# A transformer block with conditioned norms: the order of loads, modulation and first products in the first stage

## The chip, the cores and the metric

The kernel runs on one core of a Trainium2 chip. A core has TensorE (PE in the profile, with its weight loads as PEld), VectorE (DVE), ScalarE (ACT), GpSimd (POOL) and SyncE (SP), which here only issues transfers. Each engine takes its instructions in a fixed order that is set when the kernel is compiled; semaphores hold an instruction until what it needs is there. The metric is device time in microseconds, the median of several runs.

## What is computed

One transformer block on x of shape (2, 2048, 512) in float32, with 16 heads of 32 and a hidden width of 2048. A condition of 512 numbers per batch row makes six vectors (two shifts, two scales, two gates) that modulate both norms and gate both branches.

```python
mod = jax.nn.silu(condition) @ Wada + bada
sh_a, sc_a, gt_a, sh_m, sc_m, gt_m = jnp.split(mod, 6, axis=1)
xm = _layernorm(x, g1, be1) * (1.0 + sc_a[:, None, :]) + sh_a[:, None, :]
x = x + gt_a[:, None, :] * _attention(xm, Wqkv, Wproj, bproj)     # causal, 16 heads
xm = _layernorm(x, g2, be2) * (1.0 + sc_m[:, None, :]) + sh_m[:, None, :]
h = jax.nn.gelu(xm @ W1 + b1, approximate=False)
x = x + gt_m[:, None, :] * (h @ W2 + b2)
```

## The kernel before

The kernel goes through batch row 0 (queries, keys and values, then attention), batch row 1 the same way with row 0's projection among it, and then the feed-forward part for all tokens. The change is in the first stage, the queries, keys and values of row 0, nearly all of it in the work ahead of the first product.

**Groups and products.** Tokens come in groups `g` of 512 (`MT`), four 128-token tiles (`MTT`) each. The features of queries and keys come in four blocks `f` of 128. A product of tokens with weights is split in two halves each way and made with seven quarter products instead of eight; their names are A11, A12, A21 (also S4), A22, S1, S2, S3. The seven need sums of weight blocks (`weight_sum`, on POOL, L944) and sums of token halves (`token_sum`, on DVE, L997). The first unit, group 0 and f = 0, is made plainly instead, by `plain`: two sums of four N = 512 matmuls, one for queries and one for keys, so that it needs no sums (`ps_qk` in the profile). `Qkv.run` then goes through the units; after each step it calls `tick`, which prepares the next group (its token tiles' loads, stats, scaling, transposes) at set steps, and `also`, which a caller gives it.

**From tokens to xmT.** `load_x` (L919) loads a group's four token tiles on SP's queue. `stats` (L218, L221, on DVE) makes mean and variance of a tile; after the last of a group, `inv_std` makes a square root on ACT (L224) and, on DVE, its reciprocal (L225) and the shift (L226). `scaled` (L964, on ACT) normalises each tile in place. `norm` gives two tiles, half a group, to `transposed`, which transposes them on TensorE (L214, `ps_xt`) and returns `modulate`: it applies scale `a1` and shift `c1` while it writes `xmT`, even chunks on DVE (L269) and odd ones on ACT (L274).

**The modulation.** Seven small transfers on ACT's queue (L1373) bring the condition, the norms' gains and the biases as rows of one tile, `rows`; one transpose makes columns of it (`ps_c`, copied to `cols`, L1402). ACT makes Silu of the condition's columns (`sc`, L1455). `load_wada` brings two of the six slices of Wada as eight transfers on SP's queue (L1391) and their bias on POOL's. `modulation` multiplies (`ps_mod`, PE), adds the bias (`mr`, L1425, DVE) and turns the rows into columns (`ps_modt`, PE; `mod`, L1434, DVE); `scale_shift` makes `a1` and `c1` of them (L1443, L1448).

**The order.** The program is written as a sequence, and a planner orders each engine's instructions by its own costs, save those that are wrapped in `act(...)`, `mm(...)` or `transpose(...)`, which stay in the order of the program among themselves. Transfers of one queue start in their order; SP's first entries are x (four), Wada (eight), Wqkv for queries and keys (four of 512 KB, L926), Wqkv for values (four, L936).

ACT holds one table of functions at a time: changing between Sqrt and Silu is an `ACT_TABLE_LOAD`. Before, Sqrt is loaded at L136 by a dummy, Silu at L1455, and Sqrt again at L224 for group 1.

Of the kernel before, what the change touches and what calls it, by code (L numbers as in the profile page):

```python
# [17 lines left out]
P = 128  # L18
# [9 lines left out]
def dit_block_kernel(  # L28
# [107 lines left out]
    nc.scalar.activation(first, eps, AF.Sqrt)  # L136
# [99 lines left out]
    def transposed(pool_, psum, xts, n0, mv, rstd, a, c, b, dst, xns=None, share=False):  # L236
# [28 lines left out]
        def modulate(chunks=range(C)):  # L265
            for k in chunks:
                src = banks[k // per][:, k % per, :]
                if k % 2 == 0 and (share or not by_act):
                    nc.vector.tensor_scalar(  # L269
                        dst[:, k, :], src,  # L270
                        a[:, k, b : b + 1], c[:, k, b : b + 1], ALU.mult, ALU.add,
                    )
                else:
                    nc.scalar.activation(  # L274
                        dst[:, k, :], src, AF.Identity,
                        bias=c[:, k, b : b + 1], scale=a[:, k, b : b + 1],
                    )

# [619 lines left out]
    class Qkv:  # L898
# [6 lines left out]
        def __init__(self, row, qp, psum):  # L905
            self.row, self.qp, self.psum = row, qp, psum
            self.xts, self.xmT, self.loads = {}, {}, []
            self.done = set()
            self.w = qp.tile([P, 7, HK, D], F32, tag="wqk", name="wqk")
            self.t = {  # L910
                n: qp.tile([P, HK, HALF_T], F32, tag=f"t{n}", name=f"t{n}")
                for n in (S1, S2, A22)
            }

        def load_x(self, g):
            xts = []
            for t in range(MTT):
                xt = self.qp.tile([P, D], F32, tag="x", name="x", bufs=4)
                nc.sync.dma_start(xt, x_rows(self.row.b * NT + g * MTT + t))  # L919
                xts.append(xt)  # L920
            self.xts[g] = xts
# [68 lines left out]
        def token_sum(self, g, n):  # L990
# [6 lines left out]
            nc.vector.tensor_tensor(o[n], x, y, ALU.subtract)  # L997
# [88 lines left out]
        def plain(self, g, f, hp):  # L1086


            xmT, steps = self.xmT[g], []
            for which in range(2):  # L1090
                box = []
                for k in range(C):
                    def run(which=which, k=k, box=box):
                        if k == 0:
                            box.append(self.psum.tile([P, MT], F32, tag="mm", name="ps_qk"))
                        n = BASE[2 * which + k // HK][0]
                        mm(
                            box[0], self.w[:, n, k % HK, f * P : (f + 1) * P], xmT[:, k, :],
                            start=k == 0, stop=k == C - 1,
                        )  # L1100
                        if k < C - 1:
                            return
                        hi, lo = self.hi_tile(hp), self.lo_tile(hp)
                        scale = HD**-0.5 if which == 0 else 1.0
                        nc.scalar.activation(hi, box[0], AF.Copy, scale=scale)
                        nc.vector.scalar_tensor_tensor(
                            lo, box[0], scale, hi.bitcast(F32), ALU.mult, ALU.subtract
                        )
                        self.stored(g, f, which, (hi, lo))
                    steps.append(run)  # L1110
# [27 lines left out]
        def run(self, hp, also, early=()):  # L1138
# [3 lines left out]
            for g in range(NG):  # L1142
                at = [0]

                def tick():
# [214 lines left out]
    with pool("wada") as wp, pool("qkv0") as qp, pool("hl0") as hp, pool(  # L1360
        "ps_qkv0", bufs=6, space=PSUM
    ) as ps_mm:
        rows = wp.tile([n_rows, P], F32, tag="rows", name="rows")
        for r, n, src in (
# [8 lines left out]
            nc.scalar.dma_start(rows[r : r + n, :], src)  # L1373
# [76 lines left out]
        for t in range(MTT):  # L1450
# [23 lines left out]
        def also(g, n):  # L1474

            if (g, n) == (0, 7):
# [850 lines left out]
```

## Time and profile before

| | |
|---|---|
| median of 3 runs | 2256.44 us (2254.54 to 2258.32) |
| profiled execution | 2256.73 us |
| its span | 2255.0 us |
| TensorE busy | 2211.3 us (98%) |
| VectorE / ScalarE / GpSimd busy | 1535.7 / 1004.6 / 1297.9 us |
| idle of TensorE until its first product of tokens | see the rows from 0 to 18.12 us in the prediction |

A row of the timeline gives the start in us from the span's start, the length in us, the engine (SPq, ACTq: the queue on which a transfer is issued), the line, the operation, what it writes and reads, and how many instructions are merged; in brackets stands the engine's idle time before and what ended it. A row of the windows gives a stretch, its length, the busy time of PE, PEld, DVE, ACT and POOL with their instructions, the clock granted to TensorE as a share of full, the mean busy share of the DMA engines and the GB/s they moved. A float32 matmul stands as two records.

### The profile page before, as it was taken

The numbers are of one execution on the slowest core, as the hardware profiler recorded it, in microseconds if no ns is written. First come the engines' busy times: TensorE is split into PE (matmuls) and PEld (weight loads), VectorE is DVE, ScalarE is ACT, GpSimd is POOL, SyncE is SP. The second block draws the span as 40 slices with busy tenths as digits, with TensorE's granted clock in tenths as the row PEclk, the third lists the DMA queues.
The fourth block names the chain that finished last, engine by engine and source line by source line (L and its number), as shares of the span: only waits on it lengthen the run. The fifth ranks groups of instructions, "written<-read, shape, count | busy, mean of one in ns | idle before, by whom it ended". The sixth has DMA issues, their size and how long they took to land.

```text
span 2255.0 us, 33464 instructions
## 1 busy us (share of the span) xinstructions
PE 2211.3 (98%) x12057; PEld 1432.2 (64%) x12057; DVE 1535.7 (68%) x3309; ACT 1004.6 (45%) x2012; POOL 1297.9 (58%) x807
## 2 busy tenths in 40 slices
PE   7999999999999999999999999999999999999998
PEld 6777555555543587855555555345787787688687
DVE  4668766777757666777577767663685586576576
ACT  4434555555564244365656555614322422332410
POOL 4253998998983695199989898444205204304210
PEclk9999999999999999999999999999999999999999
DMA  8877143231324799542324113363353354353433
GB/s 281 251 259 193 43 93 75 62 85 48 106 97 135 252 308 313 142 92 62 85 67 104 44 48 131 109 231 129 109 175 133 123 184 145 108 187 126 158 125 110
DMA packets 160510, 311.57 MB, mean 138 GB/s; under 512 B 16544, under 2 KB 48844, under 8 KB 158552
## 3 DMA queue, kind: packets, MB, share of 16 engines
q1 hardware_dynamic: 155488, 285.53, 41.8%
q0 software_dynamic: 4480, 23.36, 2.7%
q8 instruction: 95, 1.56, 0.3%
q14 instruction: 71, 0.58, 0.1%
q10 hardware_dynamic: 376, 0.55, 0.1%
HBM read 229.95 MB, written 87.29 MB: 141 GB/s over the span
## 4 chain that ended last, share of the span: by engine, by line
PE 89%; DVE 4%; DMA 2%; POOL 2%; ACT 1%; issue 1%; SPq 0%; DVEq 0%; ACTq 0%; POOLq 0%
PE ps_a L206 27%; PE st L206 18%; PE ps_b L206 12%; PE o L206 10%; PE s L206 9%; PE ps_c L206 4%; PE ps_o L206 4%; PE sm L206 3%; DVE junk L498 1%; POOL ee L695 1%; PE ps_xt L214 1%; DMA x<-in_x_dram 1%; ACT e L670 1%; DVE mx L504 1%; PE ps_o L214 1%
## 5 line engine op out<-in xcount | busy, mean ns | idle before, releaser
L670 ACT ACTIVATE e<-st 128x512 f32<-128x512 f32 (+1 forms) x1152 | 575.0, 579 | 362.4 <-PE st L206 321.3
L504 DVE TENSOR_REDUCE mx<-s 128x1 f32<-128x512 f32 x576 | 381.9, 686 | 199.0 <-PE s L206 197.9
L695 POOL TENSOR_TENSOR ee<-ee,e 128x2048 f32<-128x2048 f32 x106 | 485.8, 4583 | 10.3 <-ACT e L670 4.3
L206 PE MATMUL st<-qst,kst 128*128 128x512 f32 (+3 forms) x1280 | 408.7, 386 | 0.0
L206 PE MATMUL s<-kst,qst 128*128 128x512 f32 (+3 forms) x1046 | 382.2, 396 | 8.0 <-DVE mx L498 2.7
L206 PE MATMUL ps_a<-sum,w 128*128 128x256 f32 (+1 forms) x1088 | 328.8, 431 | 0.1
L206 PE MATMUL o<-e,vv 128*32 128x512 f32 (+3 forms) x2560 | 293.2, 537 | 0.3 <-POOL e L682 0.3
L206 PEld LDWEIGHTS st<-qst,kst 128*128 128x128 f32 x1280 | 228.5, 188 | 97.3 <-issue 65.7
L498 DVE CUSTOM_DVE_ANT_0 junk<-s,causal 128x128 bf16<-128x128 f32 (+3 forms) x470 | 220.7, 470 | 61.0 <-PE s L206 46.8
L1795 POOL TENSOR_TENSOR sum<-w 128x256 f32<-128x256 f32 x30 | 21.8, 727 | 397.1 <-DMA w<-w1d 203.1
L206 PEld LDWEIGHTS s<-kst,qst 128*128 128x128 f32 x1046 | 195.4, 189 | 72.4 <-DVE mx L504 15.4
L206 PEld LDWEIGHTS ps_a<-sum,w 128*128 128x128 f32 x1088 | 204.5, 190 | 40.1 <-issue 11.4
L695 POOL TENSOR_TENSOR ee<-e 128x2048 f32<-128x2048 f32 x42 | 192.5, 4583 | 43.5 <-ACT e L670 42.5
L206 PEld LDWEIGHTS <-sel 32*128 32x128 bf16 x1152 | 29.5, 91 | 197.0 <-issue 196.1
L2014 ACT ACTIVATE h<-h,cols 128x512 f32<-128x512 f32 x120 | 76.8, 710 | 136.3 <-DVE h L1716 136.3
L504 DVE TENSOR_REDUCE mx<-st 128x1 f32<-128x512 f32 x192 | 131.0, 682 | 0.5
L682 POOL TENSOR_SCALAR_AFFINE_SELECT e<-e 128x512 f32<-128x512 f32 x128 | 83.3, 669 | 67.2 <-ACT e L670 67.2
L206 PE MATMUL st<-fold,sel 32*128 32x512 bf16 (+1 forms) x1152 | 117.3, 372 | 1.2
L206 PEld LDWEIGHTS o<-e,vv 128*32 128x32 f32 x2560 | 59.1, 108 | 92.3 <-issue 72.8
L1716 DVE TENSOR_TENSOR h<-c,ps_b 128x256 f32<-128x256 f32 x90 | 37.9, 421 | 103.5 <-PE ps_b L206 103.0
L1066 POOL TENSOR_TENSOR lo<-lo,hi 128x512 fp32r<-128x512 f32 x32 | 40.7, 1274 | 114.2 <-ACT hi L1064 109.8
L206 PE MATMUL ps_b<-sum,w 128*128 128x256 f32 (+1 forms) x384 | 95.0, 383 | 0.0
(237 smaller groups left out, 3590.7 us busy)
## 6 DMA issues: line engine op xcount, KB each, us to landing
qst<-q SPq DMA_DIRECT2D x128, 256.0 KB
kst<-k SPq DMA_DIRECT2D x128, 256.0 KB
w<-w1d SPq DMA_DIRECT2D x32, 896.0 KB
w<-w2d SPq DMA_DIRECT2D x28, 1024.0 KB
w<-w2d SPq DMA_DIRECT2D x28, 768.0 KB
q<-hi SPq DMA_DIRECT2D x32, 256.0 KB
q<-lo SPq DMA_DIRECT2D x32, 256.0 KB
k<-hi SPq DMA_DIRECT2D x32, 256.0 KB
```

The lines of the kernel that those rows point to most:

```text
L206: return tc.keep_in_program_order(nc.tensor.matmul(*args, **kw))
L214: return tc.keep_in_program_order(nc.tensor.transpose(dst, src, ident[:n, :n]))
L498: nc.vector.tensor_tensor_reduce(junk[:, :w], x, causal[:, QB - w :], 1.0, MASKED, ALU.add, ALU.max, m,)
L504: self.vector(nc.vector.tensor_reduce(m, x, axis=AX.X, op=ALU.max))
L670: act(nc.scalar.activation(e4[:, h, :w], sts[h][:, :w], AF.Exp))
L682: nc.gpsimd.affine_select(d, d, pattern=[[0, HC], [1, P]], compare_op=ALU.is_ge, fill=0.0, base=0, channel_multiplier=-1,)
L695: act(nc.gpsimd.tensor_tensor(dst, x, y, ALU.add))
L1066: engine.tensor_tensor(lo, d, hi.bitcast(F32), ALU.subtract)
L1716: act(nc.vector.tensor_tensor(dst, x, y, ALU.add))
L1795: act(engine.tensor_tensor(dst, u, v, op))
L2014: nc.scalar.activation(d[j], d[j], AF.Gelu, bias=col(r_b1 + half * HF + fs[j], 1))
```

## The change

1. SP's queue: the first two token tiles, then Wada, then the other two token tiles, then the weights of queries and keys by halves of the columns (f = 0, 1, then f = 2, 3), eight transfers of 256 KB, then those of values.
2. The condition has a transfer and a tile of its own (`rows_c`), ahead of the other small ones, and a transpose of its own (`ps_1`). Silu is loaded first, by a dummy behind the small transfers, and Sqrt behind Silu's use.
3. TensorE makes 6 dummy transposes ahead of `ps_1` and 32 behind it, ahead of the modulation.
4. Group 0's statistics are closed after two tiles each (`at_once`). The first half is normalised, transposed and modulated ahead of the first products; the second half's transposes and xmT, and the token sums, come after the products of the first half.
5. `plain` goes over token halves: four N = 256 matmuls for queries and four for keys with the first half of the tokens, then the same with the second.
6. The order is held (`act`) for xmT's writers, the token sums of group 0 and the stats of group 1.

```diff
-    nc.scalar.activation(first, eps, AF.Sqrt)
...
         def modulate(chunks=range(C)):
...
+                if share:
+                    act(ins)
...
-        def load_x(self, g):
+        def load_x(self, g, lo=0, hi=MTT):
...
-        def load_w(self, queue):
+        def load_w(self, queue, f=slice(0, D)):
             for n, i, k in BASE:
                 act(
                     queue.dma_start(
-                        self.w[:, n], w_v[:, k * HK : (k + 1) * HK, i * D : (i + 1) * D]
+                        self.w[:, n, :, f],
+                        w_v[:, k * HK : (k + 1) * HK, i * D + f.start : i * D + f.stop],
                     )
                 )
...
-            if t == MTT - 1:
-                inv_std(mv1, rstd1, shift1, n0, n0 + MTT)
+            if t % self.at_once == self.at_once - 1:
+                inv_std(mv1, rstd1, shift1, n0 + t + 1 - self.at_once, n0 + t + 1)
...
-            xmT, steps = self.xmT[g], []
...
+            xmT, steps, box = self.xmT[g], [], {}
+
+            def run(j, which, i):
+                tok = slice(j * HALF_T, (j + 1) * HALF_T)
+                if (j, i) == (0, 0):
+                    box[which] = self.psum.tile([P, MT], F32, tag="mm", name="ps_qk")
+                for k in range(i * HK, (i + 1) * HK):
+                    n = BASE[2 * which + i][0]
+                    mm(
+                        box[which][:, tok],
+                        self.w[:, n, k % HK, f * P : (f + 1) * P], xmT[:, k, tok],
+                        start=k == 0, stop=k == C - 1,
+                    )
+                if (j, i) != (1, 1):
+                    return
...
+            for j in range(2):
+                for which in range(2):
+                    for i in range(2):
+                        steps.append(lambda j=j, which=which, i=i: run(j, which, i))
...
-                            self.stats(g + 1, n - 10)
+                            self.stats(g + 1, n - 10, g == 0)
...
-            nc.scalar.dma_start(rows[r : r + n, :], src)
+            if not r:
+                act(nc.scalar.dma_start(rows_c, src))
+            act(nc.scalar.dma_start(rows[r : r + n, :], src))
+        act(nc.scalar.activation(first, eps, AF.Silu))
...
-        qkv.load_x(0)
+        qkv.load_x(0, 0, HK)
         load_wada(0, 1)
-        qkv.load_w(nc.sync)
+        qkv.load_x(0, HK, MTT)
+        for f0 in (0, 2):
+            qkv.load_w(nc.sync, slice(f0 * P, (f0 + 2) * P))
...
-        ps_c = ps_mm.tile([P, n_rows], F32, tag="mm", name="ps_c")
-        transpose(ps_c, rows)
-        nc.vector.tensor_copy(cols[:, :n_rows], ps_c)
+        ps_w = ps_sp.tile([P, P], F32, tag="s", name="ps_w")
+
+        def busy(n):
+            for _ in range(n):
+                transpose(ps_w, ident)
+
+        busy(6)
+        ps_1 = ps_sp.tile([P, n_cond], F32, tag="s", name="ps_1")
+        transpose(ps_1, rows_c)
...
-        for t in range(MTT):
-            qkv.stats(0, t)
-        halves = [qkv.norm(0, 0, True)]
-
         act(
             nc.scalar.activation(
-                sc[:, :, :B], col(0, n_cond).rearrange("p (b c) -> p c b", c=C), AF.Silu
+                sc[:, :, :B], ps_1.rearrange("p (b c) -> p c b", c=C), AF.Silu
             )
         )
+        act(nc.scalar.activation(first, eps, AF.Sqrt))
+        busy(32)
+        qkv.at_once = 2
+        for t in range(2):
+            qkv.stats(0, t)
+        qkv.scaled(0, 0)
         picks()
         columns = modulation(0)
-        halves.append(qkv.norm(0, 1, True))
+        ps_c = ps_mm.tile([P, n_rows], F32, tag="mm", name="ps_c")
+        transpose(ps_c, rows)
+        nc.vector.tensor_copy(cols[:, :n_rows], ps_c)
         columns()
+        modulate = qkv.norm(0, 0, True)
         scale_shift(a1, c1, r_g1, r_be1, 0, 1)
-        for k in range(0, C, 2):
-            for modulate in halves:
-                modulate((k, k + 1))
-        for n in (S1, S2, A22):
-            qkv.token_sum(0, n)
+        modulate()
+        for t in range(2, MTT):
+            qkv.stats(0, t)
+        qkv.scaled(0, 1)
+        qkv.at_once = MTT
...
         def also(g, n):
 
+            if (g, n) == (0, 2):
+                qkv.norm(0, 1, True)()
+                for s in (S1, S2, A22):
+                    qkv.token_sum(0, s, True)
```

More of the change, by code (lines that the diff above doesn't have):

```diff
@@ L268, in modulate @@
                 if k % 2 == 0 and (share or not by_act):
-                    nc.vector.tensor_scalar(
+                    ins = nc.vector.tensor_scalar(
                         dst[:, k, :], src,
@@ L273, in modulate @@
                 else:
-                    nc.scalar.activation(
+                    ins = nc.scalar.activation(
                         dst[:, k, :], src, AF.Identity,
@@ L908, in __init__ @@
             self.done = set()
+            self.at_once = MTT
             self.w = qp.tile([P, 7, HK, D], F32, tag="wqk", name="wqk")
@@ L913, in __init__ @@
             }
-        def load_x(self, g):
-            xts = []
-            for t in range(MTT):
+        def load_x(self, g, lo=0, hi=MTT):
+            xts = self.xts.setdefault(g, [])
+            for t in range(lo, hi):
                 xt = self.qp.tile([P, D], F32, tag="x", name="x", bufs=4)
@@ L920, in load_x @@
                 xts.append(xt)
-            self.xts[g] = xts
-        def load_w(self, queue):
+        def load_w(self, queue, f=slice(0, D)):
             for n, i, k in BASE:
@@ L988, in operands, with token_sum @@
             }
-        def token_sum(self, g, n):
+        def token_sum(self, g, n, keep=False):
             o = self.operands(g)
@@ L996, in token_sum @@
             }[n]
-            nc.vector.tensor_tensor(o[n], x, y, ALU.subtract)
+            ins = nc.vector.tensor_tensor(o[n], x, y, ALU.subtract)
+            if keep:
+                act(ins)
         def bank(self, name):
@@ L1086, in plain @@
         def plain(self, g, f, hp):
-            xmT, steps = self.xmT[g], []
[L1090 to L1110, printed above, removed]
+            xmT, steps, box = self.xmT[g], [], {}
@@ new lines, in run @@
+            def run(j, which, i):
[11 more added lines that the diff above has]
+                    return
+                hi, lo = self.hi_tile(hp), self.lo_tile(hp)
+                scale = HD**-0.5 if which == 0 else 1.0
+                nc.scalar.activation(hi, box[which], AF.Copy, scale=scale)
+                nc.vector.scalar_tensor_tensor(
+                    lo, box[which], scale, hi.bitcast(F32), ALU.mult, ALU.subtract
+                )
+                self.stored(g, f, which, (hi, lo))
@@ L1363, in dit_block_kernel @@
         rows = wp.tile([n_rows, P], F32, tag="rows", name="rows")
+        rows_c = wp.tile([n_cond, P], F32, tag="rowsc", name="rowsc")
         for r, n, src in (
```

1 line of the change is left out of this document (removed).

## The prediction

> **What bounds the kernel now.** I read the page first, then the instructions in order of time up to 50 us, then windows of the clock and of the DMA engines.
>
> ```profile
> span 2255.0 us, 33464 instructions
> PE 2211.3 (98%) x12057; PEld 1432.2 (64%) x12057; DVE 1535.7 (68%) x3309; ACT 1004.6 (45%) x2012; POOL 1297.9 (58%) x807
> PE 89%; DVE 4%; DMA 2%; POOL 2%; ACT 1%; issue 1%; SPq 0%; DVEq 0%; ACTq 0%; POOLq 0%
> ```
>
> TensorE (PE) carries 89% of the chain, so a late start of its steady work moves the end by as much. The change touches only the stretch before that. Its rows, all engines:
>
> ```profile
> 0.81 2.38 SPq L919 DMA_DIRECT2D x<-in_x_dram  x4
> 1.41 0.29 POOL masks.py:199 TENSOR_SCALAR_AFFINE_SELECT ident<-ident 128x128 f32<-128x128 f32 x1
> ...
> 4.22 3.79 SPq L1391 DMA_DIRECT2D vv<-in_L_cond_Wada_dram  x8
> 4.32 1.28 ACT L136 ACT_TABLE_LOAD   x1 [4.32 <-DMA x<-in_x_dram]
> ...
> 5.68 0.69 DVE L218 BATCH_NORM_STATS2 stat<-x 128x6 f32<-128x512 f32 x1 [0.38 <-DMA x<-in_x_dram]
> 6.51 0.66 DVE L218 BATCH_NORM_STATS2 stat<-x 128x6 f32<-128x512 f32 x1
> 7.30 0.19 DVE L105 CAST identb<-ident 128x128 bf16<-128x128 f32 x1
> 7.42 0.30 ACT L224 ACTIVATE rstd<-mv,eps 128x4 f32<-128x4 f32 x1 [1.61 <-DVE mv L221]
> 7.92 0.17 DVE L225 RECIPROCAL rstd<-rstd 128x4 f32<-128x4 f32 x1
> 8.12 0.16 DVE L226 SCALAR_TENSOR_TENSOR shift<-mv,rstd 128x4 f32<-128x4 f32 x1
> 8.32 1.52 ACT L964 ACTIVATE x<-x,shift,rstd 128x512 f32<-128x512 f32 x2 [0.60 <-DVE shift L226]
> 9.89 1.76 PE L214 MATMUL ps_xt<-ident,x 128*128 128x128 f32 x7 [0.23 <-ACT x L964]
> 11.58 2.75 PE L206 MATMUL ps_mod<-vv,sc 128*32 128x512 f32 x16
> 12.89 0.12 PEld L206 LDWEIGHTS ps_mod<-vv,sc 128*32 128x32 f32 x1 [0.26 <-DMA vv<-in_L_cond_Wada_dram]
> 14.26 1.09 PE L214 MATMUL ps_xt<-ident,x 128*128 128x128 f32 x8
> 14.54 0.69 DVE L1425 TENSOR_TENSOR mr<-ps_mod,mr 128x512 f32<-128x512 f32 x1 [6.26 <-PE ps_mod L206]
> 15.29 1.05 PE L206 MATMUL ps_modt<-pickc,mr 128*128 128x4 f32 x8
> 17.07 1.90 DVE L269 TENSOR_SCALAR xmT<-ps_xt,a,c 128x256 f32<-128x256 f32 x4
> 18.12 7.13 PE L206 MATMUL ps_qk<-xmT,wqk 128*128 128x512 f32 x16 [1.78 <-DVE xmT L269]
> 18.43 10.36 POOL L944 TENSOR_TENSOR wqk<-wqk 128x256 f32<-128x256 f32 x12 [0.18 <-DMA wqk<-in_L_cond_Wqkv_dram]
> 21.89 0.95 DVE L1472 COPY pick<-pickc 128x512 f32<-128x512 f32 x1
> 25.09 1.03 PE L206 MATMUL ps_a<-xmT,wqk 128*128 128x256 f32 x4
> 25.91 1.28 ACT L224 ACT_TABLE_LOAD   x1
> 27.40 0.36 ACT L1059 ACTIVATE lo<-ps_a 128x256 f32<-128x256 f32 x1
> 27.86 1.10 PE L206 MATMUL ps_a<-t,wqk 128*128 128x256 f32 x4 [0.89 <-POOL wqk L944]
> 28.80 1.03 PE L206 MATMUL ps_b<-xmT,wqk 128*128 128x256 f32 x4
> ```
>
> Four things are to be seen. The first products (ps_qk) begin at 18.12, and ahead of them runs one chain: the last load of Wada lands by 12.89, ps_mod, the add mr at 14.54, modt, a and c, xmT. Second, the 0.89 idle at 27.86 is put down to POOL, but ACT's copy of ps_a, which had to leave before that bank was accumulated further, ran from 27.40 to 27.76, behind a table load: that copy is the true releaser. Third, VectorE (DVE) keeps its order: ident was ready at 1.70, yet the cast at 7.30 stood behind stats that waited for tiles of x. Fourth, the transposes at 9.89 took 0.25 each, those at 14.26 0.136: TensorE was still slow at the first.
>
> **Transfers.** SP moves the last two token tiles from ahead of the eight Wada loads to behind them.
>
> ```profile
> 2.10:12.89 10.79, 3.78 (x17) 2.11 (x20) 4.14 (x16) 6.21 (x9) 3.31 (x8) 1.00 0.95 321
> 12.89:18.30 5.41, 3.63 (x29) 2.26 (x23) 2.51 (x8) 0.59 (x2) 1.55 (x3) 1.00 1.06 389
> ```
>
> The DMA engines are full (0.95, 1.06), so place in the queue decides: a load of 262 KB costs 0.67 at 389 GB/s. Wada's last load becomes the tenth and lands at 12.89 - 2 x 0.67 = 11.5; the fourth token tile becomes the twelfth and lands where Wada's did, 12.89. One more small transfer and waits on ACT's queue push Silu's table load from 4.32 to perhaps 5.1, sc to about 6.8: cover 4.7 us until 11.5, so nothing; without that cover, the same microseconds. The eight halves of wqk follow; POOL's sums for f = 1 can start near 16 instead of 18.43, well ahead of their products, so nothing. The 38 dummy transposes take at most 38 x 0.25 = 9.5 from about 2 and end before 12: ps_mod (2.75 at worst) then ends by 14.7, which is not last, as follows.
>
> **The new wait.** The compiled order on DVE after its opening copies is this (ordinary text, not profile):
>
> ```
> pickc; stat x2; aggr; rstd (half 0); stat x3; shift (half 0); aggr;
> rstd (half 1); shift (half 1); pick; mr<-ps_mod,mr; cols; mod<-ps_modt; a; c; c; xmT ...
> ACT: sc; table load; sqrt half 0; first; scale x0, x1; sqrt half 1; scale x2, x3; xmT ...
> PE: ps_w x6; ps_1; ps_w x32; ps_mod; ps_c; ps_modt; ps_xt half 0; 8 products; ps_xt half 1; 8 products
> ```
>
> So shift of half 0 stands behind the statistics of the very last tile, and mr behind half 1's rstd, which waits for ACT's sqrt, which stands behind the scaling of x0 and x1. Step by step: the two stats start 0.83 apart (5.68, 6.51) and the last tile lands at 12.89, so stat x3 runs 13.05 to 13.71; shift to ACT 0.20 (8.12 to 8.32), scaling from 13.93 to 15.45 (1.52); sqrt to reciprocal 0.50 (7.42 to 7.92): 15.95; shift 16.15; pick 16.31, 0.95 (now ahead of mr; a lower end is 0.69, the mr add on as many columns, the higher the row); mr at 17.26 against 14.54. From mr to the first product it was 3.58; a half needs one xmT chunk less (1.90 / 4 = 0.47): 3.11. First product at 20.37, **2.25 late**. Who waits for DVE: PE, with modt and all of ps_xt behind it.
>
> **The clock.** PE then idles from about 12 to 18.0. What shorter idles did:
>
> ```profile
> 117.10:119.10 2.00, 0.01 (x1) 0.00 (x0) 1.06 (x3) 0.00 (x0) 0.00 (x0) 1.00 1.03 384
> 119.20:125.90 6.70, 6.04 (x14) 4.87 (x15) 5.10 (x15) 0.82 (x2) 2.27 (x3) 0.50 0.58 199
> 119.86 0.80 PE L206 MATMUL s<-kst,qst 128*128 128x512 f32 x1 [2.75 <-DVE mx L498]
> ...
> 876.68 0.33 PE L214 MATMUL ps_xt<-ident,x 128*128 128x128 f32 x1 [3.79 <-ACT x L964]
> 876.90:880.20 3.30, 2.92 (x11) 2.55 (x11) 0.60 (x1) 3.02 (x7) 3.22 (x5) 0.50 0.99 193
> ```
>
> An idle of 2.75 brought 6.7 us at half clock (0.50), one of 3.79 brought 3.3. With 6 us I expect half clock from 18.0 on. modt at the ratio of the transposes (0.25 / 0.136 = 1.85) takes 1.94, ps_xt 2.0: products from about 21.7 if the clock returns after 3.4, **1.35 more** (bounds: 0, and 1.6 if it stays low), and 0 to 1.45 in the products (half of 21.9 to 24.8, for the longer slow time), of which I take **0.3**, as the row after the longer idle is the nearer. [...]
>
> [...]
>
> **Products by halves.** Eight N = 256 products take 8 x 0.43 = 3.47 (25.09 to 28.80 shows 0.87 for two); both halves 6.94, as ps_qk's 6.97 (18.12 to 25.09). But half 1's eight transposes now stand between them, 0.87, with 0.2 for the first xmT chunk: **1.05 later**. They were hidden before.
>
> **Gains.** The table load at 25.91 goes (Sqrt now stays loaded after Silu), and with it the idle: **0.89 earlier** (between 0 and 0.89). Late next would be the token sums on DVE: three of 0.8 to 1.1 after the last xmT, done some 2 us before use.
>
> **Group 1.** The kept order puts its shift on DVE behind the combine of feature 2's S4, the product just ahead of the group's transposes. The trace shows this pattern one group later:
>
> ```profile
> 36.57 1.04 PE L214 MATMUL ps_xt<-ident,x 128*128 128x128 f32 x8
> 77.02 0.16 DVE L226 SCALAR_TENSOR_TENSOR shift<-mv,rstd 128x4 f32<-128x4 f32 x1
> ...
> 78.08 0.33 PE L214 MATMUL ps_xt<-ident,x 128*128 128x128 f32 x1 [1.01 <-ACT x L964]
> 78.79 0.98 PE L214 MATMUL ps_xt<-ident,x 128*128 128x128 f32 x7 [0.38 <-ACT x L964]
> ```
>
> The transposes at 36.57 did not wait; now I expect 1.01 + 0.38 = **1.4 later** (0 to 1.7). Transfers of group 1 and the second Wada pair change places in SP's queue, with no wait of PE there now: nothing, or at most a load's 0.67 each way.
>
> **Sum.** 2.25 + 1.35 + 0.3 + 1.05 - 0.89 + 1.4 = 5.5 later. The profiled execution took 2256.73, 1.7 beyond its span and 0.3 above the median of 2256.44; so 2262.2 on it, 2261.9 against the median; I say 2261.8.
>
> **Rivals.** *It does what it says*: the late tiles do not hold mr. For it: 11.5 + 1.65 (12.89 to 14.54) puts mr at 13.15, the first product at 16.26, 1.86 early; with 1.05 and -0.89 that is 1.7 faster, 2254.7: not slower. Against it is the order on DVE. It decides where the last tile lands 3.8 us before my 12.89, near 9.1: then all but the clock is paid. *The clock stays full*: 2.25 + 1.05 - 0.89 + 1.4 = 3.8, 2260.2; against it, both idles above. *Group 1 does not wait*: 4.1, 2260.5; for it, a shift queued behind combines cost nothing at 36.57. *A second slow stretch*: an added idle near 40 or a longer one near 117 halves the clock for 6.7 more, 3.4 us of work: 2265.2.
>
> **How the numbers follow.** Forecast 0.48, in 2260 to 2264; as it says 0.15; clock full 0.13; group 1 without a wait 0.12; second slow stretch 0.12. 0.2%, 4.5 us, is about what a measurement can tell from no change, so slower begins at 2260.9: 0.42 of the forecast, 0.12, and a third of the two middling cases, 0.60. Faster needs the first rival and the loss of the slow stretch at 119 (3.4) together: 0.04. Same: 0.36. The range, 2254.5 to 2266.5, reaches from the first rival's time to the last one's with the longer slow clock.
>
> **What would show it.** Right: stat x3 near 13, mr near 17.3, first product near 21.7, a granted clock of 0.50 near 18 to 21, ACT without a third table load, ps_xt of group 1 waiting for ACT. Wrong: mr before 15, or a first product before 18.

## The result, and the profile after

| | before | after |
|---|---|---|
| median, measured side by side on one chip, 21 runs each | 2257.89 us (2253.47 to 2260.11) | 2260.92 us (2258.71 to 2262.94) |
| ratio, with its 95% interval | | 1.0015 [1.0009, 1.0021] |
| profiled execution, and its span | 2256.73, 2255.0 us | 2259.23, 2257.5 us |

The changed kernel is 3.0 us slower, 0.15%. The forecast was 2261.8, 5.4 above the median known then. Direction and range hold; the way there does not, as the traces show. The prediction took 0.2% as about the least that a measurement can tell; here the interval is 0.06% to either side, so 0.15% is told from no change. From the page of the changed kernel, the span and the busy times:

```profile
span 2257.5 us, 33580 instructions
...
PE 2219.3 (98%) x12112; PEld 1440.7 (64%) x12112; DVE 1534.4 (68%) x3311; ACT 1003.7 (44%) x2013; POOL 1296.0 (57%) x807
```

It looks much like that of before. TensorE's busy time is 8.0 us longer, but 6.75 of that are the dummy transposes (5.21 and 1.54), so where the loss arises can't be read there. The timeline of the changed kernel from the last token tiles to group 1's transposes (start, length, engine, line, operation, and in brackets the idle time before with what ended it):

```profile
13.38 0.69 DVE L217 BATCH_NORM_STATS2 stat<-x 128x6 f32<-128x512 f32 x1 [7.50 <-DMA x<-in_x_dram]
...
14.26 0.67 DVE L217 BATCH_NORM_STATS2 stat<-x 128x6 f32<-128x512 f32 x1
...
15.02 1.52 ACT L966 ACTIVATE x<-x,shift,rstd 128x512 f32<-128x512 f32 x2 [6.95 <-DVE shift L225]
...
16.76 0.17 DVE L224 RECIPROCAL rstd<-rstd 128x2 f32<-128x2 f32 x1 [1.62 <-ACT rstd L223]
...
17.04 0.42 DVE L1498 COPY pick<-pickc 128x512 f32<-128x512 f32 x1
...
17.38 0.68 DVE L1446 TENSOR_TENSOR mr<-ps_mod,mr 128x512 f32<-128x512 f32 x1
...
18.11 1.87 PE L205 MATMUL ps_modt<-pickc,mr 128*128 128x4 f32 x8 [4.12 <-DVE mr L1446]
...
19.84 1.95 PE L213 MATMUL ps_xt<-ident,x 128*128 128x128 f32 x8
...
21.58 4.71 PE L205 MATMUL ps_qk<-xmT,wqk 128*128 128x256 f32 x16
...
26.12 1.04 PE L213 MATMUL ps_xt<-ident,x 128*128 128x128 f32 x8
...
27.36 3.89 PE L205 MATMUL ps_qk<-xmT,wqk 128*128 128x256 f32 x16 [0.20 <-DVE xmT L268]
...
31.08 1.03 PE L205 MATMUL ps_a<-xmT,wqk 128*128 128x256 f32 x4
...
32.81 1.03 PE L205 MATMUL ps_a<-t,wqk 128*128 128x256 f32 x4
...
42.66 0.33 PE L213 MATMUL ps_xt<-ident,x 128*128 128x128 f32 x1 [1.05 <-ACT x L966]
...
43.37 0.98 PE L213 MATMUL ps_xt<-ident,x 128*128 128x128 f32 x7 [0.38 <-ACT x L966]
```

The chain is the one that was forecast: stats of the late tiles, shift, scaling of the first half, the second half's square root and reciprocal, pick, and only then mr; TensorE stands idle for 4.12 us. From within this wait on, the clock is at one half, as this window of the changed kernel shows (length, busy time and instructions of PE, PEld, DVE, ACT, POOL, granted clock, share and GB/s of the DMA engines); the records of the clock give 0.50 from 16.79 to 23.62:

```profile
16.80:23.60 6.80, 5.49 (x21) 4.93 (x22) 3.01 (x11) 2.65 (x4) 6.03 (x10) 0.50 0.98 294
```

Up to here the changed kernel falls behind: the first product starts 3.46 later than before (21.58 against 18.12), ps_a<-t 4.95 (32.81 against 27.86), group 1's transposes 6.09 (42.66 against 36.57). That delay does not reach the end. Timeline and one window of the changed kernel near 117 us, where scores of the attention (s) come between the products:

```profile
115.04 1.97 SPq L1239 DMA_DIRECT2D kst<-in_L_cond_W_dram  x4
117.11 1.84 SPq L921 DMA_DIRECT2D x<-in_x_dram  x4
...
117.57 0.82 PE L205 MATMUL s<-kst,qst 128*128 128x512 f32 x2
...
126.11 0.50 PE L205 MATMUL s<-kst,qst 128*128 128x512 f32 x1 [0.23 <-DVE mx L505]
...
129.40 0.48 PE L205 MATMUL s<-kst,qst 128*128 128x512 f32 x1
```

```profile
112.00:115.00 3.00, 1.74 (x9) 1.21 (x8) 1.39 (x2) 1.55 (x4) 0.00 (x0) 1.00 0.10 36
```

The same work in the kernel before:

```profile
107.57 4.91 SPq L1230 DMA_DIRECT2D kst<-in_L_cond_W_dram  x4
...
110.10 0.81 PE L206 MATMUL s<-kst,qst 128*128 128x512 f32 x2
...
112.58 1.84 SPq L919 DMA_DIRECT2D x<-in_x_dram  x4
...
115.91 0.69 DVE L218 BATCH_NORM_STATS2 stat<-x 128x6 f32<-128x512 f32 x1 [2.07 <-DMA x<-in_x_dram]
...
127.00 0.48 PE L206 MATMUL s<-kst,qst 128*128 128x512 f32 x1
```

```profile
106.30:111.60 5.30, 4.87 (x23) 4.23 (x23) 2.97 (x7) 1.38 (x4) 1.76 (x2) 1.00 0.94 330
```

The pair of scores at 110.10 comes 7.47 later (117.57), the single one at 127.00 only 2.40 later (129.40): 5.1 us are given back in between. Before, SP asks for weights of the feed-forward part (kst) and then for the next group's tokens (x) while the DMA engines are full (0.94): its issues take 4.91, VectorE waits 2.07 for a tile, the scores' maxima stand behind those statistics, TensorE waits the 2.75 at 119.86 that the prediction quotes, and 6.8 us at half clock follow. In the changed kernel kst is asked for 7.5 later and x 4.5 later, and kst meets nearly empty DMA engines (0.10): its issues take 1.97, the longest wait of TensorE among the scores is 0.23, and the clock stays full. The score that waited 2.75 at 119.86 stands at 124.52 there, 4.7 later: so 2.8 of the 5.1 are the wait and 2.3 the half clock behind it. What is also under way on the DMA engines before, a store of 896 KB (w1d) that GpSimd issues at 106.22 and that lands 5.4 us later, is issued at 106.77 in the changed kernel and lands 4.0 later: it did not move with TensorE. From there on the two traces stay 1.9 to 2.8 apart, 2.5 at the end.

### The profile page after: what moved, and what is told of

It is laid out like the page before. It is cut to its first block, busy times and chain, and to the rows that moved or that the text cites. A ratio compares the mean times of both kernels' runs of the same rounds, so it can differ in the third digit from the quotient of the medians.

```text
span 2257.5 us, 33580 instructions
## 1 busy us (share of the span) xinstructions
PE 2219.3 (98%) x12112; PEld 1440.7 (64%) x12112; DVE 1534.4 (68%) x3311; ACT 1003.7 (44%) x2013; POOL 1296.0 (57%) x807
## 4 chain that ended last, share of the span: by engine, by line
PE 87%; DVE 3%; POOL 2%; ACT 1%; DMA 1%; issue 1%; SPq 0%; DVEq 0%; ACTq 0%; POOLq 0%
PE ps_a L205 25%; PE st L205 18%; PE ps_b L205 11%; PE o L205 10%; PE s L205 9%; PE ps_c L205 4%; PE ps_o L205 4%; PE sm L205 3%; POOL ee L696 1%; DVE junk L499 1%; PE ps_xt L213 1%; ACT e L671 1%; DVE mx L505 1%; PE ps_o L213 1%; DMA x<-in_x_dram 0%
## 5 line engine op out<-in xcount | busy, mean ns | idle before, releaser
L696 POOL TENSOR_TENSOR ee<-ee,e 128x2048 f32<-128x2048 f32 x106 | 485.8, 4583 | 10.6 <-ACT e L671 4.6
```

What stands on the lines that cost most here:

```text
L696: act(nc.gpsimd.tensor_tensor(dst, x, y, ALU.add))
```

## Experiments

The times of each group were taken beside the kernel before on the same chip (medians 2257.03, 2257.74, 2257.62 and 2257.35 us in the four groups). "Late by" is against the trace of before: the start of group 1's transposes (36.57), the pair of scores (110.10), the one score (127.00), and the spans. The ratio is the recorded one and need not be that of the two medians. The last four columns come from one execution of each kernel: before_one, which reaches 110 us within 0.2 of the kernel before, is 1.9 ahead at 127, so differences of some 2 us there say little.

| kernel | median | ratio to before | late at 36.57 | at 110.10 | at 127.00 | span |
|---|---|---|---|---|---|---|
| the changed kernel | 2260.92 | 1.0015 [1.0009, 1.0021] | 6.1 | 7.5 | 2.4 | +2.5 |
| late_start | 2258.53 | 1.0004 [0.9996, 1.0013] | 5.4 | 3.8 | -0.4 | +0.7 |
| late_start2 | 2265.90 | 1.0036 [1.0022, 1.0049] | 14.2 | 12.3 | 8.4 | +9.6 |
| early_x | 2258.02 | 1.0005 [0.9994, 1.0016] | 0.1 | 0.2 | -4.3 | -4.2 |
| mr_first | 2259.25 | 1.0010 [1.0002, 1.0019] | 3.0 | 4.8 | 0.6 | +2.5 |
| no_dummies | 2260.78 | 1.0013 [1.0005, 1.0022] | 6.4 | 9.7 | 4.6 | +5.3 |
| stay_warm | 2262.19 | 1.0020 [1.0012, 1.0029] | 8.4 | 8.9 | 4.1 | +4.1 |
| no_keep | 2260.25 | 1.0011 [1.0003, 1.0020] | 5.7 | 5.8 | 0.8 | +1.8 |
| tables_only | 2267.35 | 1.0037 [1.0022, 1.0051] | 9.0 | 7.7 | 7.1 | +10.6 |
| tables_one | 2260.03 | 1.0007 [0.9998, 1.0017] | 4.3 | 5.1 | 1.4 | +3.2 |
| early_x_one | 2256.13 | 0.9989 [0.9980, 0.9998] | 1.8 | 1.8 | -2.4 | -0.9 |
| mr_ex_one | 2256.56 | 0.9993 [0.9984, 1.0001] | 3.9 | 5.8 | 0.2 | -0.3 |
| before_one | 2257.01 | 0.9999 [0.9990, 1.0009] | 0.1 | 0.2 | -1.9 | +0.1 |

### Is a late start given back? (late_start, late_start2)

The kernel before, with nothing changed but dummy transposes between the modulation and the first product. The theory was that near 117 us a wait for transfers takes up a delay of TensorE; the rival, and the prediction's own step, that the delay lasts to the end.

```diff
         scale_shift(a1, c1, r_g1, r_be1, 0, 1)
+        ps_w = ps_sp.tile([P, P], F32, tag="s", name="ps_w")
+        for _ in range(72):          # late_start2: 144
+            transpose(ps_w, ident)
```

> The kernel before with 72 dummy transposes between the modulation and the first product, about 7.8 us on TensorE, of which 1.8 fall into its idle time: the first product comes near 24.2, 6.1 us late, and nothing else is changed. Theory A (the first stage's delay is given back near 117 us, where the kernel before waits for a transfer that does not move with TensorE): the wait of 2.75 us and its half clock are gone, and the end is at most 2.5 us later, ratio 1.000 to 1.001. Rival B (the changed order of group 1 is what took that wait away): the wait stays and the end is 5 to 6 us later, ratio 1.0025.

> As late_start, with 144 dummy transposes instead of 72: the first product comes near 32.5, 14.4 us late. Theory (the wait near 117 us and its half clock, 6.2 us in the profile of before, are all that can be given back): 8 to 9 us of it are left at the end, ratio 1.0035 to 1.004. Rival (the transfers carry several waits that shrink one after the other): less than 6 us are left.

Timeline of late_start:

```profile
24.75 7.03 PE L206 MATMUL ps_qk<-xmT,wqk 128*128 128x512 f32 x16
...
121.75 0.50 PE L206 MATMUL s<-kst,qst 128*128 128x512 f32 x1 [0.83 <-DVE mx L498]
...
126.64 0.48 PE L206 MATMUL s<-kst,qst 128*128 128x512 f32 x1
```

The first product comes 6.6 later (24.75), yet the score of 127.00 comes at 126.64: the whole delay is gone. The wait of 2.75 has become 0.83, and no half clock follows. The larger dose, 14.2 late at group 1's transposes, still is 8.4 late behind 127 and 9.6 at the end. So the give-back is real and has a limit: late_start2 lost 5.8 of its 14.2 by 127, late_start all of 5.4. Not all of it is lost near 117: 1.9 of each is gone by 82 us, behind group 2's transposes, which wait 1.01 and 0.38 in the kernel before (78.08) and not in late_start; 4.2 and 3.9 are given back between 110.10 and 127.00. The medians agree: late_start's interval allows 2.9 us at most of the 6.6. The rival is refuted; the prediction's sentence that a late start "moves the end by as much" is wrong for delays of this size.

### What makes the wait near 117? (early_x)

The kernel before, with the next group's tokens asked for three steps earlier.

```diff
-                        if n == 3 and g + 1 not in self.xts:
+                        if n == 0 and g + 1 not in self.xts:
                             self.load_x(g + 1)
```

> The kernel before with the next group's token tiles asked for at a group's first step instead of its fourth, so that they stand ahead of the feed-forward weights in SP's queue. Theory A (that wait near 117 us comes from the tiles' place in the queue): the 2.75 us and the 6.8 us at half clock go, and the end is 4 to 6.5 us earlier, ratio 0.9971 to 0.9982. Rival (the tiles land late wherever they stand, because the transfers are full): the wait stays over 1.5 us and the end is within 1.5 us of the kernel before.

Timeline of early_x:

```profile
107.75 4.94 SPq L919 DMA_DIRECT2D x<-in_x_dram  x4
112.80 1.92 SPq L1230 DMA_DIRECT2D kst<-in_L_cond_W_dram  x4
...
115.28 1.92 PE L206 MATMUL ps_mod<-vv,sc 128*32 128x512 f32 x16 [1.11 <-DVE mx L504]
```

In the trace the theory holds: the wait of 2.75 is 1.11, no half clock follows, and 4.3 us are gained by 127. By the median it fell: 4 to 6.5 us were forecast, and the median is no lower than before (2258.02, from 2252.55 to 2265.08). The execution that was profiled was its fastest, so what the wait near 117 costs a usual execution of the kernel before stays open. The trace also corrects my reading of the slow issue: whichever request stands first at 107.6 takes 4.9, kst or x, so it is no wait for kst's own buffer. What both share is the full DMA engines (0.99 from 109 to 112 in both traces), with the store of 896 KB (w1d) under way since 106. That this store is the cause was not tried by itself, but the traces sort by it. In the five in which the first of SP's requests for kst and x comes 1.3 to 1.6 us behind the store (before, before_one, early_x, early_x_one, tables_only), that request takes 1.21 to 1.25; in the other nine it comes 3.2 us or more behind and takes 0.39 to 0.46. Waits of TensorE of 2 us or more among the scores there stand only in before, before_one and tables_only.

### Was the order on VectorE the loss? (mr_first)

The changed kernel, with the last two tiles' stats held behind the bias add.

```diff
-            def columns():
+            def columns(then=None):
                 nc.vector.tensor_tensor(mr, ps, mr, ALU.add)
+                if then:
+                    then()                    # stats of tiles 2 and 3, order held
...
-        for t in range(2, MTT):
-            qkv.stats(0, t)
         qkv.scaled(0, 1)
```

> The changed kernel with the statistics of its last two token tiles put behind the modulation's add. Theory (the order on VectorE holds the modulation): the add comes at about 14 instead of 17.4, the clock stays full, the first product near 17.3 instead of 21.6, and ps_a<-t,wqk of f = 1 near 27 instead of 32.8. If something else held it, the first product stays near 21. For the end: if the delay is given back near 117 us, the wait there comes back and the end is within 2.5 us of the kernel before, 2 to 4 us ahead of the changed kernel; if every microsecond of the start counts, it is 5.8 us ahead of the changed kernel.

Timeline of mr_first:

```profile
14.09 0.69 DVE L1446 TENSOR_TENSOR mr<-ps_mod,mr 128x512 f32<-128x512 f32 x1 [5.88 <-PE ps_mod L205]
...
17.82 3.89 PE L205 MATMUL ps_qk<-xmT,wqk 128*128 128x256 f32 x16 [1.00 <-DVE xmT L268]
...
28.23 1.03 PE L205 MATMUL ps_a<-t,wqk 128*128 128x256 f32 x4
...
39.56 0.33 PE L213 MATMUL ps_xt<-ident,x 128*128 128x128 f32 x1 [2.50 <-ACT x L966]
```

The add mr stands at 14.09 and no longer at 17.38, and the first product comes 3.8 earlier than in the changed kernel, at full clock, so the order on VectorE was the whole of that loss. Even so, the first product is only 0.3 ahead of the kernel before, and at ps_a<-t nothing is left (28.23 against 27.86): from the first product to ps_a the halves take 8.68 (17.82 to 26.50) where the kernel before took 6.97, and these 1.71 are more than the 0.30 won at the start and the 1.04 of the table load. Then group 1's transposes wait 2.50 instead of 1.05, half clock follows from 40.16 to 43.57, and the span ends where that of the changed kernel does (2257.5). For the median 2 to 4 us less than the changed kernel were expected; the two intervals overlap (1.0002 to 1.0019, 1.0009 to 1.0021), so no gain is shown.

### The dummy transposes (no_dummies, stay_warm)

The first leaves out the 38 dummies of the changed kernel, the second adds 36 ahead of modt, to keep TensorE at full clock through its wait.

```diff
-        busy(6)                     # no_dummies
-        busy(32)                    # no_dummies
+        busy(36)                    # stay_warm, ahead of columns()
```

> The changed kernel without its 38 dummy transposes. Theory (their warm clock is lost again before the first products, and Wada's landing sets the end of the modulation's products): the products end within 1 us of where they did (13.8), the add stays near 17.4 and the first product within 0.5 us of 21.6; the end within 1 us of the changed kernel. Rival (they matter): the first product is 1.5 us or more later.

> The changed kernel with 36 more dummy transposes in TensorE's idle stretch behind the modulation's products. Theory (the idle of 4.1 us brought the half clock): the granted clock stays 1.00 from 14 to 24, modt takes 1.05 instead of 1.87, the first product comes near 20.4 instead of 21.6, and the first eight products take 3.5 instead of 4.5; the second half starts 2.2 us earlier. [...] The end: 0 to 2.2 us ahead of the changed kernel.

Timeline of no_dummies:

```profile
20.46 6.44 PE L205 MATMUL ps_qk<-xmT,wqk 128*128 128x256 f32 x16 [1.05 <-DVE xmT L268]
...
26.74 1.04 PE L213 MATMUL ps_xt<-ident,x 128*128 128x128 f32 x8
```

Timeline of stay_warm:

```profile
20.57 5.47 PE L205 MATMUL ps_qk<-xmT,wqk 128*128 128x256 f32 x16 [0.88 <-DVE xmT L268]
...
35.09 1.10 PE L205 MATMUL ps_a<-t,wqk 128*128 128x256 f32 x4 [2.36 <-DVE t L999]
```

The median shows no worth of the 38 dummies: 2260.78 without them and 2260.92 with them. But the run leaves out more than the dummies. Without them the clock is first on record as full at 26.01, and the first eight products take 6.28 (20.46 to 26.74) against 4.54 (21.58 to 26.12); they start earlier, because the planner then put mr ahead of the second half's reciprocal (14.98 and 16.29). I had expected mr and the first product to stay where they were. In stay_warm modt runs at full clock, as I expected, but half clock comes all the same, from 21.00 to 24.41, after an idle of only 0.88; and the token sums now release ps_a<-t late (2.36). My expectation of a gain fell.

### Group 1's held order (no_keep)

```diff
-                            self.stats(g + 1, n - 10, g == 0)
+                            self.stats(g + 1, n - 10)
```

> The changed kernel with the order of group 1's statistics left to the planner, which then puts the first two between the xmT of the first and of the second half. Theory (group 1's transposes wait because its statistics stand late on VectorE): the waits of 1.05 and 0.38 us near 43 us are gone and that point comes 1.4 us earlier. At the end 0 to 1.4 us earlier than the changed kernel, nearer to 0 if delays are given back near 117 us. Rival (ACT or the transfers of the tokens hold them): the wait stays over 1 us.

Timeline of no_keep:

```profile
39.51 1.10 PE L205 MATMUL ps_a<-t,wqk 128*128 128x256 f32 x4 [1.06 <-ACT lo L1063]
...
42.24 1.04 PE L213 MATMUL ps_xt<-ident,x 128*128 128x128 f32 x8
```

The wait ahead of the transposes is gone, and 1.06 stands in its place three products earlier, behind the same scalings on ACT. In the medians the two can't be told apart (2260.25 and 2260.92).

### The order of the tables alone (tables_only, tables_one)

The kernel before with part 2 of the change alone: the condition's own transfer and transpose, Silu first and Sqrt behind it.

```diff
-    nc.scalar.activation(first, eps, AF.Sqrt)
...
+            if not r:
+                act(nc.scalar.dma_start(rows_c, src))
+            act(nc.scalar.dma_start(rows[r : r + n, :], src))
+        act(nc.scalar.activation(first, eps, AF.Silu))
...
-                sc[:, :, :B], col(0, n_cond).rearrange("p (b c) -> p c b", c=C), AF.Silu
+                sc[:, :, :B], ps_1.rearrange("p (b c) -> p c b", c=C), AF.Silu
...
+        act(nc.scalar.activation(first, eps, AF.Sqrt))
```

> The kernel before with only the second part of the change: the condition's own transfer and transpose, Silu's table first, Sqrt's behind it, no dummy transposes, tokens and products whole as before. Theory: the third table load is gone and with it the 0.89 us ahead of the first ps_a<-t,wqk; the modulation's products end at the landing of Wada's last load plus about 1.1 us instead of 1.4, so the first product comes 0 to 0.5 us earlier and ps_a<-t,wqk 0.9 to 1.4 us earlier than 27.86. Rival (the 0.89 us was POOL's, as the profile put it): the wait stays. For the end: if an early start is lost again near 117 us, the end is within 0.7 us of the kernel before; if not, 0.9 to 1.4 us earlier.

It was the slowest of all, 2267.35, and I had no term for that. Timeline of tables_only:

```profile
30.78 3.91 DVE L225 SCALAR_TENSOR_TENSOR shift<-mv,rstd 128x4 f32<-128x4 f32 x1
...
30.98 3.69 POOL L948 TENSOR_TENSOR wv<-wv 128x512 f32<-128x512 f32 x3
...
36.01 1.36 PE L205 MATMUL ps_b<-xmT,wqk 128*128 128x256 f32 x4 [4.11 <-ACT lo L1058]
```

An instruction on four columns took 3.91, as long as three of GpSimd's sums, and ended with the third of them; ACT's scaling and its copy of ps_b stood behind it, TensorE behind those.

The same trace is the one in which a delay was not given back, 7.7 late at 110.10 and 7.1 at 127.00:

```profile
113.94 0.57 POOL L1266 DMA_DIRECT2D w1d<-qst  x1 [0.30 <-POOL qst L1250]
...
115.29 5.33 SPq L1229 DMA_DIRECT2D kst<-in_L_cond_W_dram  x4
...
128.25 0.50 PE L205 MATMUL s<-kst,qst 128*128 128x512 f32 x1 [3.42 <-DVE mx L497]
```

Here the store was late by as much as the requests (113.94 for 106.22, 115.29 for 107.57). They met as in the kernel before, the wait is 3.42, and half clock follows from 128.87 to 132.29.

For the shift, tables_one makes it from one tensor at a time:

```diff
-        nc.vector.scalar_tensor_tensor(
-            shift[:, lo:hi], mv[:, lo:hi, 0], -1.0, rstd[:, lo:hi], ALU.mult, ALU.mult
-        )
+        for n in range(lo, hi):
+            nc.vector.tensor_scalar(
+                shift[:, n : n + 1], mv[:, n, 0:1], rstd[:, n : n + 1], -1.0, ALU.mult, ALU.mult
+            )
```

> The table order alone (tables_only), with the shift made by one tensor_scalar for each tile (the reciprocal as a pointer to one value per partition) in place of one scalar_tensor_tensor of two tensors. Theory: in tables_only the shift of group 1 took 3.91 us at 30.78 (0.26 in the kernel before) because an instruction of VectorE with two tensors of SBUF is held while GpSimd works in SBUF, and GpSimd's sums follow one another without a gap there; with one tensor it is not held: the four small instructions take under 0.6 together, the wait of 4.11 us ahead of ps_b at 36.01 falls below 1, the delay against the kernel before at group 1's transposes goes from 9.0 to about 5, and the time from 2267.4 to 2258 to 2263 (late_start, 5.4 late at the same place, ended at 2258.5). Rival: the shift was long for another cause (a semaphore, the order of the planner): the wait of about 4 stays, 2265 to 2269.

Timeline of tables_one:

```profile
29.77 0.30 ACT L223 ACTIVATE rstd<-mv,eps 128x4 f32<-128x4 f32 x1 [3.26 <-DVE mv L220]
...
30.43 0.58 DVE L226 TENSOR_SCALAR shift<-mv,rstd 128x1 f32<-128x1 f32 x4
30.44 1.85 PE L205 MATMUL ps_a<-t,wqk 128*128 128x256 f32 x4 [2.83 <-POOL wqk L944]
...
30.62 3.72 POOL L949 TENSOR_TENSOR wv<-wv 128x512 f32<-128x512 f32 x3
```

Beside the same sums of GpSimd the four instructions, each made from one tensor, took 0.58 and were not held, and the time went to 2260.03 as the theory had it. Not all of those 7.3 us are the shift's: in tables_only the first product was already 1.46 later (20.20 against 18.74). The wait ahead of ps_b is gone, as expected, but 2.83 stand one product earlier, ahead of ps_a<-t. The row names GpSimd, whose sum had ended at 29.43; ACT's copy of ps_a stood from 29.97 to 30.33 behind the square root of group 1, which waited for VectorE's statistics until 29.77. So in this run the table load that goes is worth nothing by itself: its place is taken by the wait for the statistics. In the changed kernel that square root comes at 40.07, and the gain is there.

### What would beat both (early_x_one, before_one, mr_ex_one)

early_x_one is early_x with the shift of tables_one, before_one the shift alone, mr_ex_one is mr_first with both edits.

> The kernel before with the next group's tokens asked for earlier (early_x) and the shift from one tensor at a time. Theory: at 871 the shift falls from 0.70 to 0.4 or less, the wait ahead of the transposes there from 3.63 to about 3.3, the half clock that follows stays; about 0.5 us less than early_x, so 2257 to 2258, no different from the kernel before by what its median can tell. [...]

> The kernel before with nothing changed but the shift, made from one tensor at a time: tells which of its two edits gave early_x_one its 1.5 us. Theory (the transfer asked for earlier gave it, the shift only the 0.2 to 0.3 us ahead of the transposes at 877): the wait of 3.79 at 876.68 goes to 3.2 to 3.6, the wait of 2.75 at 119.86 stays, and the time is within 1 us of the kernel before, 2256.6 to 2258.6. Rival (the shift gave it, by more places than those seen): 2256.5 or below, with a wait of under 1.5 us near 120.

> mr_first with the next group's tokens asked for earlier and the shift from one tensor at a time: the candidate to beat both. Theory: the first product stays near 17.8; the wait of 2.50 us ahead of group 1's transposes stays over 1.5, since it comes from the statistics that stand behind the token sums (4.31 us for two) and not from the shift (0.15); the end within 1.5 us of mr_first, 2258 to 2260. Rival (the transfer of the tokens sets group 1's statistics): the wait falls under 1, no half clock near 40, and the time 2254 to 2256.

early_x_one is the one kernel whose interval lies below the kernel before, 0.11% [0.02%, 0.20%], and it is below the changed kernel too. Its 2256.13 lies 0.9 below the 2257 to 2258 that I had expected, and one interval out of twelve that ends so near to no change can be chance. If it is a gain, which edit gives it stays open: alone, neither moved the median (1.0005 and 0.9999, with intervals that overlap that of both together). before_one had its wait at 876.68 go from 3.79 to 3.24 as expected, but also the 2.75 to 2.03, which I had expected to stay. mr_ex_one is the change with its late order mended: 2256.56, lower than the changed kernel by some 0.2% (the intervals 0.9984 to 1.0001 and 1.0009 to 1.0021 do not meet), not different from the kernel before. Its wait ahead of group 1's transposes, 1.59, stayed over 1.5 as the theory had it, and the time fell between theory and rival.

## Why the prediction was right or wrong

- **The chain to mr.** Right in its order, with mr at 17.38 for 17.26. That it came so near is luck, as sizes that were off cancelled: the last stats began at 14.26 for 13.05, since the third tile was there only at 13.38, while pick held mr for 0.34 and not 0.95, and the reciprocal came 0.22 behind the scaling (16.54 to 16.76) and not 0.50.
- **The clock and the first product.** Right: half clock from 16.79 to 23.62, first product at 21.58 for 21.7, so 3.46 for 2.25 + 1.35. But the half clock lasted 6.83, where the prediction took 3.4, as it lasted behind the longer idle of the kernel before (3.41, from 876.87 to 880.28); what that cost is in the next point. mr_first shows by taking the order away that it was the cause.
- **Products by halves.** Mis-sized, 2.53 for 0.3 + 1.05. ps_qk of before took 6.97 from first to next product, here 9.50 (21.58 to 31.08): transposes between the halves 1.24, slow clock 0.82 (4.54 against 3.72 for the second half), and 0.47 because a half takes 3.72 and not the 3.47 that I read off the row of N = 256 products.
- **The third table load.** Right in the changed kernel, 1.04 earlier for 0.89 (from ps_a to ps_a<-t 1.73, before 2.77). Before, ACT's loads stand at 4.32, 9.86 and 25.91, 1.28 each; in the changed kernel at 4.81 and 6.39, and none ahead of group 1's square root at 40.07. tables_only and tables_one show that it holds only where the square root is not late.
- **Group 1.** Right in kind, 1.05 + 0.38 of waiting for 1.4; with the lone matmuls' ends 1.79 (the products behind start 6.74 later, from 4.95). no_keep shows that the held order decides only where the wait stands.
- **The sum.** These come to 6.74 for 5.5, and some 0.7 more is added by 110 us (0.53 of it a wait at 92.67). By its own step "a late start of its steady work moves the end by as much" the time would have been some 2264.
- **The step that failed is this one.** A stretch that is paced by transfers stands near 117: 5.1 of 7.5 us were given back there, and 4.2 of a bare delay in late_start. In tables_only, where the store was late as well, it was not given back. The prediction had the rows of that stretch, 2.75 and 6.70, and used them only as an example of the clock; it named the loss of that slow stretch only beside the first rival. Two errors of opposite sign, 2.0 too little up to 110 and 5.1 too much after, turn the forecast 5.5 into 2.4, against 2.5 in the trace and 3.0 in the medians. The forecast time is only 0.9 above the measured one because the kernel before also measured 1.5 higher beside the changed one than in the runs shown before. That nearness is luck.
- **The rivals.** "It does what it says" and "the clock stays full" were refuted by mr at 17.38 and the clock of 0.50. "Group 1 does not wait" was refuted by 1.05. "A second slow stretch" went the other way: one was lost.

## What to carry to other kernels

Before a delay ahead of the steady work is carried to the end, look along the bound engine's row for the next wait that is paced by something which the delay does not move, here transfers: that wait can take up the delay, and a half-clocked stretch behind it can go with it (of the 5.1 us here, 2.8 were the wait and 2.3 the half clock). The trace of tables_only, where that other work was late too, suggests that it holds only as long as the other work stays put. Whether a faster start is lost at the same place was not tried: no run reached group 1's transposes ahead of the kernel before. And look at what the fixed order puts ahead of the one instruction that the next engine waits for: statistics of tiles that come late had no business ahead of mr (17.38 behind them, 14.09 ahead of them).

## What the runs showed of the hardware that was not expected

**The granted clock changed only at marks 3.41 us apart.** In all fourteen traces every change of the granted clock lies a whole number of 3.413 us from the first one of that trace, up to 659 of them later (the changed kernel: 16.79, 23.62, 880.36, 883.78, 2255.93). From the rows I worked out TensorE's idle time between two marks at full clock: leaving out the end of the kernel, all 22 such stretches with more than 1.92 us of it were followed by half clock; from 1.78 to 1.92 two of four were; below that only three, all among the short instructions ahead of the first product (0.96 in stay_warm). So here the same wait cost half clock or not by where the marks fell. The windows of early_x_one:

```profile
15.95:19.30 3.35, 1.57 (x8) 1.00 (x8) 2.73 (x9) 1.50 (x4) 1.83 (x4) 1.00 1.07 371
19.40:22.70 3.30, 3.30 (x5) 1.30 (x4) 3.16 (x4) 0.33 (x1) 3.22 (x4) 0.50 1.08 369
```

and the same windows of the kernel before:

```profile
15.95:19.30 3.35, 1.57 (x7) 0.98 (x7) 2.81 (x9) 1.59 (x4) 2.43 (x5) 1.00 1.07 368
19.40:22.70 3.30, 3.30 (x9) 1.51 (x8) 3.16 (x4) 0.84 (x2) 3.22 (x4) 1.00 1.08 373
```

Both wait 1.78 ahead of the first product. In early_x_one it lies between the marks at 15.93 and 19.35, and 3.4 us at 0.50 follow; before, a mark at 16.71 cuts it, 1.41 lie on one side, and the clock stays full. The executions of one kernel differ in their clock too: of the 105 of the kernel before that were timed beside the experiments, the 16 with a mean granted clock of 0.996 had a median of 2260.66 us, the 41 at 0.998 one of 2256.76 and the 13 at 0.999 one of 2254.53. That it is the place of the marks which differs between them is read from the two traces here, not shown for the rest. So one trace's gain of 4.2 (early_x) need not be the median's.

**An instruction of VectorE was held for several of GpSimd's.** The shift of group 1, made from two tensors, took 3.91 in tables_only, where it takes 0.16 with GpSimd idle (8.27 in the same trace); three of GpSimd's sums in a row went ahead (3.69 of the 3.91). Made from one tensor, four instructions took 0.58 beside such sums (tables_one). The trace of before has more of it. Its token sums t<-xmT,t, from two tensors, took 0.69 where GpSimd did not work (54.93, 909.00) and 3.59 at 751.85, beside three of GpSimd's instructions; lo<-ps_b,lo, of which one tensor is a product's sum, took 0.39 to 0.43 in all 31 cases, GpSimd at work or not. But lo<-lo,hi at 57.86 was not held (0.69 beside sums of GpSimd), and xn, made from one tensor and two columns, took 1.50 at 1460.98 and 0.53 at 1495.80: so the number of tensors alone does not tell when it happens. The token sums of the changed kernel, which read two tensors beside GpSimd's sums, took 1.53 for the first and 3.25 for the next two, where before they took 0.81 and 2.16; that this has the same cause is read from the rows and was not tried.
